# A smaller edge matrix and one-hots for four groups at once, in a four-layer graph network on one core

## The chip, the cores and the metric

The kernel runs on one core of a Trainium2 chip. Its time is the device time of one execution in microseconds (us); three executions of the kernel before took 3287.37, 3274.63 and 3283.2 us, a median of 3283.2 us. All rows of the profile come from one further execution that the hardware profiler recorded.

## What is computed

The reference runs four graph layers over 6250 nodes of 128 features and 106250 edges, which are sorted by their destination. Each layer is followed by a residual addition and a layer norm:

```python
x = _layernorm(x + _L0_gnn_ref(x, edge_attr_128, src, dst, ...))   # sums of edge features per destination, two dense layers
x = _layernorm(x + _L1_gnn_ref(x, edge_index, ...))                # sums of neighbours' rows, two dense layers with batch norms
x = _layernorm(x + _L2_gnn_ref(x, edge_index, ...))                # means of neighbours' rows, twice
x = _layernorm(x + _L3_gnn_ref(x, edge_index, edge_attr_16, ...))  # attention over the edges, three heads
```

What matters here is one expression. It is needed three times (once in the second layer and twice in the third):

```python
agg = jax.ops.segment_sum(x[src], dst, num_segments=n)
```

For each destination the rows of all its sources are added up, 17 on average. The edges are the same each time; only x differs.

## The kernel before

**Two ways to the sums.** The destinations are divided at ND = 5000 (line 45). For the first 5000 the kernel multiplies by a matrix: entry (s, d) is the number of edges from node s to destination d. It is built once, in bf16, kept in DRAM in ND/500 = 10 parts of 500 destinations ("edges", the list `matrix`), and read back by each of the three neighbour sums. For the other 1250 destinations the sources' rows are fetched from a table in DRAM, one indirect DMA of GpSimd (POOL) for 128 edges, and multiplied by one-hots of the destinations. The edges of these are in window groups of three such tiles; four groups make a quad, and the fetched quads are those from Q0 = 54 on: 183 tiles.

**Stage 0, the keys (to 101 us).** For each edge slot `key` gets a number that tells the block of the source and its destination within a group of GD = 5, and `low` the place of the source within its block. A group of five destinations fills one column of both tiles.

**Stage 1, layer 0's edge sums and the build (101 to 517 us).** The loop over `batches` (70) loads four window groups of edge features, makes their one-hots on VectorE (`one_hots`, line 352), multiplies them on TensorE (`by_group`, line 341), moves the result by ScalarE (line 343), and adds it to the layer's sums on VectorE (line 348). From the seventh batch on each turn advances `making` (from line 610) by some steps. One step of it is four groups: for each group VectorE compares a row of numbers with one column of `low` (`olow`, 128 wide, line 632) and another with one column of `key` (`okey`, 250 wide, line 634), TensorE multiplies the two one-hots (`made`, line 635), which counts the edges of 128 sources-in-block by 250 (block, destination) pairs, and ScalarE casts the four results from PSUM into the stage in the arena (line 637). 50 groups make a slice of SC = 250 destinations, that is 13 steps, the last with two groups; two slices make a part. A finished slice goes to DRAM in five DMAs on ScalarE's queue (line 618), 625 KB each. The pool `mk`, from which `olow` and `okey` come, has 8 buffers of each.

**Stages 2 to 4, `neighbours` (from line 770), called once for each sum.** Its outer loop runs over the matrix's parts, its inner one over ten pieces of each part. A piece is a DMA of 625 KB on SyncE's queue (five buffers) and 15 matmuls (line 837: five blocks by three, since the bf16 rows are split into three terms). After a piece, the generator `gathered` is advanced where the list `due` names that piece, so that the quads of the fetched destinations are spread over the pieces. One quad issues the fetches of the next quad (12, line 792; the `rows` pool holds two quads), makes one-hots, multiplies 24 times (`both`), and adds the result to `accg`. The spreading is in two lines:

```python
last = n_pieces * after // dense - 6
due = [(i + 2) * last // (2 * len(quads) + 2) for i in range(2 * len(quads))]
```

`after` is the number of parts after which the quads' destinations are finished (`others`): all of them in the first two calls, all but two in the third. `before`, `take`, `then` and `late` are the layer's own work on a part of 500 destinations, and `each` is work that is done once for a piece. In the first call `each` advances generators that load the 16-wide edge features on POOL's queue (lines 683 and 685, `eat`) and count edges (`counting`, lines 522 to 545, with an iota on POOL at line 540); in the second call it issues 50 indirect DMAs on POOL's queue (`last_sums`, line 657, `st`). In the third call `then` scatters each part's `edst` by four indirect DMAs on POOL's queue (line 1063).

**Stage 5, the attention (2300 to 3562 us),** gathers from x and uses neither the matrix nor the one-hots of the build.

What sets the order: each engine runs its instructions in the order in which the program issues them. POOL issues all indirect DMAs and works through them one by one; a fetch for quad q+1 can start when TensorE has used the rows of quad q-1.

Of the kernel before, what the change touches and what calls it, by code (L numbers as in the profile page):

```python
# [8 lines left out]
F32 = mybir.dt.float32  # L9
I32 = mybir.dt.int32  # L10
AF = mybir.ActivationFunctionType
OP = mybir.AluOpType
# [7 lines left out]
F = 128  # L20
# [18 lines left out]
RT, RB = 7, 119  # L39
GT, NG, GW = 3, 277, 32  # L40
BT, NBT, BW = 4, 208, 40
PB, NB5 = 125, 50
GD = 5
SC = 250
ND, Q0 = 5000, 54
AN = N - ND + SC + GW
BF16 = mybir.dt.bfloat16
ROUND = 12582912.0
# [7 lines left out]
def gnn_kernel(ctx: ExitStack, tc: tile.TileContext, a: dict, out: bass.AP):  # L56
# [142 lines left out]
    with tc.If(ordered) as cond:  # L199
        by_windows(tc, a, out, consts, ix)  # L200
# [9 lines left out]
def by_windows(ctx: ExitStack, tc: tile.TileContext, a: dict, out: bass.AP, consts, ix):  # L210


    nc = tc.nc
    iota, part, ident, ones, epst = consts
# [103 lines left out]
    def bases(at, n, engine, last=N - 1):  # L318

        got = {}  # L320

        def of(g):
            if g % 4 == 0:
                m = min(4, n - g)
                _, v = nc.values_load_multi_w_load_instructions(
                    ix["base"][0:1, at + g:at + g + m], engines=[engine], min_val=0, max_val=last,
                    skip_runtime_bounds_check_because=WITHIN)
                got.update({g + i: y for i, y in enumerate(v)})
            return got[g]
        return of  # L330
# [29 lines left out]
    arena = wide.tile([128, 2 * NB5 * SC], BF16, name="arena")  # L360
# [10 lines left out]
    def split(x, blocks, pool):  # L371
# [13 lines left out]
    keep = ExitStack()  # L385
    keyp = keep.enter_context(tc.tile_pool(name="keys", bufs=1))
    GP = 1024
    key = keyp.tile([128, GP], F32, name="key")
    low = keyp.tile([128, GP], F32, name="low")
    iob = keyp.tile([128, 128], BF16, name="iob")  # L390
    nc.vector.tensor_copy(iob, iota)
    iok = keyp.tile([128, NB5 * GD], BF16, name="iok")
    nc.gpsimd.iota(iok, pattern=[[1, NB5 * GD]], base=1, channel_multiplier=0,
                   allow_small_or_imprecise_dtypes=True)
    GC = GP // 128

    eap = keep.enter_context(tc.tile_pool(name="ea", bufs=4))
    ohp = keep.enter_context(tc.tile_pool(name="oh", bufs=3))
    mkp = keep.enter_context(tc.tile_pool(name="mk", bufs=8))
    evp = keep.enter_context(tc.tile_pool(name="ev", bufs=2))  # L400
    gw = keep.enter_context(tc.tile_pool(name="gw", bufs=1))
    pp = keep.enter_context(tc.tile_pool(name="sps", bufs=2, space=bass.MemoryType.PSUM))
# [24 lines left out]
    def start_row(r0, tg):  # L427
        nc.vector.tensor_scalar(r0, tg, 128.0, -128.0, op0=OP.mult, op1=OP.add)
        nc.vector.tensor_scalar(r0, r0, 0.0, float(E - 128), op0=OP.max, op1=OP.min)
# [9 lines left out]
    def by_c(x):  # L439
# [9 lines left out]
                   allow_small_or_imprecise_dtypes=True)  # L449
# [4 lines left out]
    for c in range(GC):  # L454
        for k in range(RT):
            nc.tensor.matmul(counts[:, c:c + 1], lhsT=below[:, k, c * 128:(c + 1) * 128], rhs=oneb,
                             start=(k == 0), stop=(k == RT - 1))
# [6 lines left out]
    s = gw.tile([128, GC], F32, name="s")  # L464
# [19 lines left out]
    s = a["L3_gnn_att_edge"]  # L484
# [12 lines left out]
    for cs in HALVES:  # L497
# [14 lines left out]
        for x, to in ((hi, key), (sf, low)):  # L512
            for c0 in range(cs.start, cs.stop, 4):
                n = min(4, cs.stop - c0)
                p = mps.tile([128, 4, 256], F32, name="made")
# [4 lines left out]
    M = 5  # L520

    def counting(pool, psum):


        row = tail[:RB, AN:AN + M * PB]
        view = arena[:RB, NB5 * 3 * F + 2 * (AN + M * PB):]
        steps = NB5 // M
        for c in range(steps + 1):
            if c:
                cs = slice((c - 1) * M, c * M)  # L530
                below = view[:, (c - 1) % 2 * M * PB:((c - 1) % 2 + 1) * M * PB]
                p = psum.tile([128, 2 * SC], F32, name="hp1")
                for i in range(M):
                    nc.tensor.matmul(p[:PB, i:i + 1], lhsT=below[:, i * PB:(i + 1) * PB], rhs=oneb,
                                     start=True, stop=True)
                start_row(n0[:PB, cs], p[:PB, 0:M])
                nc.vector.tensor_copy(n0i[:PB, cs], n0[:PB, cs])
            if c < steps:
                below = view[:, c % 2 * M * PB:(c % 2 + 1) * M * PB]
                nc.gpsimd.iota(row, pattern=[[1, M * PB]], base=c * M * PB + 1, channel_multiplier=0,  # L540
                               allow_small_or_imprecise_dtypes=True)
                nc.vector.tensor_scalar(below, row, ix["df"][:, 0:1], None, op0=OP.is_gt)
                for k in range(1, RT):
                    nc.vector.scalar_tensor_tensor(below, row, ix["df"][:, k:k + 1], below, op0=OP.is_gt, op1=OP.add)
            yield
# [34 lines left out]
    def products():  # L580
# [26 lines left out]
        nc.vector.tensor_add(cb, p, linb)  # L607
        yield

    def making(pool, psum):  # L610


        per = SC // GD
        full_of = []

        def store(i):
            s, w = full_of[0], NB5 * SC // 5
            nc.scalar.dma_start(matrix[s // 2][s % 2, :, i * w:(i + 1) * w],
                                stage[:, s % 2, :, :].rearrange("p h c -> p (h c)")[:, i * w:(i + 1) * w])
            if i == 4:  # L620
                full_of.pop()

        for s in range(ND // SC):
            for q in range(0, per, 4):
                if full_of and q // 4 in (1, 3, 5, 7, 9):
                    store(q // 8)
                n = min(4, per - q)
                p = psum.tile([128, 4, 256], F32, name="made")
                for i in range(n):
                    g = s * per + q + i  # L630
                    o = pool.tile([128, 128], BF16, name="olow")
                    nc.vector.tensor_scalar(o, iob, low[:, g:g + 1], None, op0=OP.is_equal)  # L632
                    w = pool.tile([128, NB5 * GD], BF16, name="okey")
                    nc.vector.tensor_scalar(w, iok, key[:, g:g + 1], None, op0=OP.is_equal)  # L634
                    nc.tensor.matmul(p[:, i, 0:NB5 * GD], lhsT=o, rhs=w, start=True, stop=True)  # L635
                to = stage[:, s % 2, :, q * GD:(q + n) * GD].rearrange("p h (i d) -> p i h d", d=GD)
                nc.scalar.copy(to, p[:, 0:n, 0:NB5 * GD].rearrange("p i (h d) -> p i h d", d=GD))  # L637
                yield
            full_of.append(s)
        for i in range(5):  # L640
            store(i)
# [53 lines left out]
    ea = a["edge_attr_128"]  # L695
    of = bases(0, NG, DVE)
    make = making(mkp, mps)
    product = products()
    quads, batches, LATE = ND // SC * 13, (NG + 3) // 4, 6
    for q in range(batches):  # L700
# [4 lines left out]
        n = min(4 * GT * 128, E - e0)  # L705
# [7 lines left out]
        p = pp.tile([128, F], F32, name="sums")  # L713
# [14 lines left out]
    with tc.tile_pool(name="l0w", bufs=2) as work, \  # L728
# [5 lines left out]
        for blocks in CHUNKS:  # L734
            b0, nb = blocks[0], len(blocks)
            w = nb * PB
# [16 lines left out]
            for j in range(nb):  # L753
                for m in range(4):
                    nc.tensor.matmul(yp[:PB, j, :], lhsT=ht[:, m, j * PB:(j + 1) * PB], rhs=w2[:, m, :],
                                     start=(m == 0), stop=(m == 3))
# [103 lines left out]
    with tc.tile_pool(name="l1", bufs=1) as wp:  # L860
# [5 lines left out]
        s = a["L1_gnn_eps"]  # L866
# [31 lines left out]
        with tc.tile_pool(name="l1d", bufs=1) as dp, tc.tile_pool(name="l1e", bufs=4) as two, \  # L898
                tc.tile_pool(name="hps", bufs=4, space=bass.MemoryType.PSUM) as hps:
            def take(k, p):  # L900
                nc.vector.scalar_tensor_tensor(h0[:, cols(k)], xt[:, cols(k)], eps1, p, op0=OP.mult, op1=OP.add)

            def then(k):
                for m in range(2):
                    stats(s1[:, m], k, hidden(k, m, hps))

            logit, indices = logits(dp, two), counting(dp, hps)

            def each(i):
                if i % 7 == 1:  # L910
                    next(indices, None)
                if i % 3 == 2:
                    next(logit, None)

            neighbours(None, take, then, tables[0], len(matrix), each)
            for x in (logit, indices):
                for _ in x:
                    pass
# [3 lines left out]
        with tc.tile_pool(name="l1p", bufs=1) as lp, tc.tile_pool(name="l1w", bufs=2) as work, \  # L922
# [4 lines left out]
            for k in range(len(PARTS)):  # L927
                h = work.tile([128, 2, 2 * SC], F32, name="h1")
                x = h0[:, cols(k)]
                w = x.shape[1]  # L930
# [11 lines left out]
        with tc.tile_pool(name="l1x", bufs=2) as work, tc.tile_pool(name="zps", bufs=3, space=bass.MemoryType.PSUM) as zps, \  # L942
                tc.tile_pool(name="tps", bufs=2, space=bass.MemoryType.PSUM) as tp:
            last = None
            for blocks in CHUNKS:
# [3 lines left out]
                                               op0=OP.mult, op1=OP.add)  # L949
# [961 lines left out]
```

## Time and profile before

| what | value |
|---|---|
| median of three timed executions | 3283.2 us |
| the profiled execution, and its span | 3564.17 us, 3562.0 us |
| granted TensorE clock over the span | 0.83 |
| stage 1 (keys ready to the last part written) | 101 to 517 us |
| first, second and third neighbour sum, with what is computed on them | 680 to 1062, 1204 to 1713, 1717 to 2184 us |
| attention | 2300 to 3562 us |

The profiled execution took 281 us longer than the median, so its rows are read for their proportions as well as for their durations. The costliest groups of instructions that the change touches:

```profile
L837 PE MATMUL sums<-piece,arena 125*128 125x500 bf16 x4500 | 1033.2, 384 | 66.3 <-issue 55.4
...
L792 POOL DMA_INDIRECT row<-table,srca x549 | 542.2, 988 | 317.8 <-issue 140.2
...
L637 ACT CAST arena<-made 128x1000 bf16<-128x1000 f32 (+1 forms) x260 | 313.5, 1261 | 61.3 <-PE made L635 52.7
...
L635 PE MATMUL made<-okey,olow 128*128 128x250 bf16 x1000 | 250.4, 329 | 59.5 <-ACT arena L637 26.2
L634 DVE TENSOR_SCALAR okey<-iok,key 128x250 bf16<-128x250 bf16 x1000 | 287.7, 288 | 0.0
...
L632 DVE TENSOR_SCALAR olow<-iob,low 128x128 bf16<-128x128 bf16 x1000 | 252.8, 253 | 0.0
```

A row names the line, the engine, the operation, the tiles written and read, the size and the number of instructions; then the busy time of all (us) and the mean of one (ns); then the engine's idle time before them, with what ended most of it. PE is TensorE, DVE VectorE, ACT ScalarE, POOL GpSimd and SP SyncE. The DMA issues of the edge matrix are these:

```profile
piece<-edges SPq DMA_DIRECT2D x300, 625.0 KB
edges<-arena ACTq DMA_DIRECT2D x100, 625.0 KB
```

### The profile page before, as it was taken

Reading aid. Unit: us, or ns where it says so; the run is one execution under the profiler, and the core shown is the slowest. Engines: PE = TensorE matmul, PEld = TensorE weight load, DVE = VectorE, ACT = ScalarE, POOL = GpSimd, SP = SyncE. Lnnn points to the kernel's source line nnn. Section 1 sums busy time; section 2 is a strip of 40 time slices with the busy share of each in tenths; the row PEclk is TensorE's granted clock in tenths of the full one; section 3 lists DMA queues with packets and bytes.
Section 4 is the critical chain, followed back from the end, with each engine's and each line's share of the span. In section 5 each row is a group of like instructions: output and inputs, shape, how many; then the busy total and the mean of one; then the engine's idle time right before and its main releaser. Section 6 shows DMA issues by size and latency. Waiting matters only on the chain.

```text
span 3562.0 us, 44386 instructions
## 1 busy us (share of the span) xinstructions
PE 2686.3 (75%) x14960; PEld 1638.6 (46%) x14960; DVE 1840.3 (52%) x6114; ACT 912.8 (26%) x1661; POOL 1693.8 (48%) x1689
## 2 busy tenths in 40 slices
PE   2788879799996479999787895566666666766665
PEld 1343436444443234445343342455555555655555
DVE  4999985387217400000211122666666666666666
ACT  0678864200005100001100010122222222222222
POOL 4000001277606475440466524666666666666663
PEclk8677789999997579999898997777777777777778
DMA  5588861387642346654454554122222222222221
GB/s 166 194 277 277 276 225 42 108 259 230 214 153 66 94 109 213 186 185 122 151 177 152 173 174 118 50 60 56 60 59 58 57 57 57 59 60 56 58 59 38
DMA packets 334840, 461.91 MB, mean 130 GB/s; under 512 B 45310, under 2 KB 219166, under 8 KB 334245
## 3 DMA queue, kind: packets, MB, share of 16 engines
q1 hardware_dynamic: 251420, 278.88, 26.0%
q0 software_dynamic: 54912, 105.86, 11.2%
q10 hardware_dynamic: 28270, 74.24, 5.7%
q8 instruction: 120, 1.97, 0.2%
q14 instruction: 118, 0.97, 0.1%
HBM read 375.30 MB, written 83.36 MB: 129 GB/s over the span
## 4 chain that ended last, share of the span: by engine, by line
PE 38%; DVE 10%; issue 10%; POOL 4%; another core or an unknown queue 3%; DMA 2%; ACT 1%; DVEq 0%; ACTq 0%; SPq 0%; POOLq 0%
PE sums L837 16%; PE o L1190 9%; PE w_p L1168 4%; PE o L1140 2%; POOL row L792 2%; DVE mx L1171 1%; PE yp L1012 1%; DVE w L1178 1%; POOL st L657 1%; PE both L1175 1%; DVE w L1163 1%; PE fp L1124 1%; PE both L341 1%; ACT w L1180 1%
## 5 line engine op out<-in xcount | busy, mean ns | idle before, releaser
L837 PE MATMUL sums<-piece,arena 125*128 125x500 bf16 x4500 | 1033.2, 384 | 66.3 <-issue 55.4
L1082 POOL DMA_INDIRECT rows<-x,srca x831 | 863.2, 1039 | 452.5 <-issue 215.1
L837 PEld LDWEIGHTS <-arena 125*128 125x128 bf16 x4500 | 436.6, 98 | 617.5 <-issue 153.9
L792 POOL DMA_INDIRECT row<-table,srca x549 | 542.2, 988 | 317.8 <-issue 140.2
L1190 PE MATMUL o<-rows,w 128*120 128x132 f32 x2078 | 406.5, 340 | 153.9 <-issue 78.6
L1190 PEld LDWEIGHTS o<-rows,w 128*120 128x120 f32 x2078 | 355.9, 239 | 192.6 <-issue 97.2
L637 ACT CAST arena<-made 128x1000 bf16<-128x1000 f32 (+1 forms) x260 | 313.5, 1261 | 61.3 <-PE made L635 52.7
L1180 ACT ACTIVATE w<-w 128x720 f32<-128x720 f32 x208 | 167.0, 803 | 610.0 <-DVE w L1178 464.8
L635 PE MATMUL made<-okey,olow 128*128 128x250 bf16 x1000 | 250.4, 329 | 59.5 <-ACT arena L637 26.2
L634 DVE TENSOR_SCALAR okey<-iok,key 128x250 bf16<-128x250 bf16 x1000 | 287.7, 288 | 0.0
L1171 DVE TENSOR_REDUCE mx<-w_p 120x1 f32<-120x768 f32 x208 | 198.0, 952 | 172.9 <-PE o L1190 76.0
L632 DVE TENSOR_SCALAR olow<-iob,low 128x128 bf16<-128x128 bf16 x1000 | 252.8, 253 | 0.0
L1168 PE MATMUL w_p<-ident,w 128*120 128x128 f32 x1248 | 231.0, 328 | 13.1 <-issue 6.3
L1178 DVE TENSOR_TENSOR w<-w,both 128x720 f32<-128x720 f32 x208 | 187.0, 899 | 81.5 <-PE w_p L1168 46.9
L352 DVE TENSOR_TENSOR onehot<-iota,relg 128x384 f32<-128x384 f32 x118 | 64.2, 546 | 309.2 <-PE both L341 183.3
L1175 PE MATMUL both<-ident,mx 120*128 120x120 f32 x208 | 74.5, 358 | 194.5 <-DVE acc L1198 121.8
L343 ACT COPY by_node<-both 128x128 f32<-128x128 f32 (+1 forms) x48 | 12.7, 266 | 810.5 <-PE both L341 531.3
L1168 PEld LDWEIGHTS w_p<-ident,w 128*120 128x120 f32 x1248 | 187.4, 169 | 56.8 <-issue 22.1
L635 PEld LDWEIGHTS <-olow 128*128 128x128 bf16 x1000 | 107.5, 113 | 184.7 <-DVE okey L634 91.2
L1163 DVE TENSOR_TENSOR w<-oh,z 128x720 f32<-128x720 f32 x208 | 187.3, 901 | 9.6 <-PE o L1190 8.3
L708 POOL MEMSET ea<- 128x128 f32 x1 | 0.5, 533 | 397.8 <-PE sums L341 397.8
L1140 PE MATMUL o<-zeros 128*120 128x380 bf16 x416 | 143.0, 396 | 23.9 <-issue 9.7
(286 smaller groups left out, 3308.6 us busy)
## 6 DMA issues: line engine op xcount, KB each, us to landing
piece<-edges SPq DMA_DIRECT2D x300, 625.0 KB
edges<-arena ACTq DMA_DIRECT2D x100, 625.0 KB
ea<-in_edge_attr_dram SPq DMA_DIRECT2D x69, 768.0 KB
loop<-x SPq DMA_DIRECT2D x208, 68.0 KB
rows<-x,srca POOLq DMA_INDIRECT x831
row<-table,srca POOLq DMA_INDIRECT x549
eat<-in_edge_attr_dram POOLq DMA_DIRECT2D x28, 236.0 KB
table<-xn SPq DMA_DIRECT2D x24, 224.0 KB
```

The source lines that it names most:

```text
L632: nc.vector.tensor_scalar(o, iob, low[:, g:g + 1], None, op0=OP.is_equal)
L634: nc.vector.tensor_scalar(w, iok, key[:, g:g + 1], None, op0=OP.is_equal)
L635: nc.tensor.matmul(p[:, i, 0:NB5 * GD], lhsT=o, rhs=w, start=True, stop=True)
L637: nc.scalar.copy(to, p[:, 0:n, 0:NB5 * GD].rearrange("p i (h d) -> p i h d", d=GD))
L792: nc.gpsimd.indirect_dma_start(out=r[:, j, :], out_offset=None, in_=table, in_offset=bass.IndirectOffsetOnAxis(ap=ix["src"][:, t:t + 1], a ...
L837: nc.tensor.matmul(p, lhsT=xp[:PB, h, i, :], rhs=t[:PB, :, (h - h0) * SC:(h - h0 + 1) * SC], start=(h == 0 and i == 0), stop=(h == NB5 - 1 ...
L1082: nc.gpsimd.indirect_dma_start(out=r[:, j, :], out_offset=None, in_=x3, in_offset=bass.IndirectOffsetOnAxis(ap=ix["src"][:, BT * b + j:BT ...
L1163: nc.vector.tensor_tensor(w, oh.to_broadcast([128, S, H, BW]), z.rearrange("p j (h w) -> p j h w", w=1).to_broadcast([128, S, H, BW]), op= ...
L1168: nc.tensor.transpose(tp[:, j // 3, j % 3 * 128:(j % 3 + 1) * 128], w[:, j, :, :].rearrange("p h w -> p (h w)"), ident)
L1171: nc.vector.tensor_reduce(mx, tp[:, :, 0:384], AX.XY, OP.max)
L1178: nc.vector.tensor_tensor(wf, wf, mb.rearrange("p (j h) w -> p j (h w)", j=1) .to_broadcast([128, S, H * BW]), op=OP.subtract)
L1190: nc.tensor.matmul(o[:, 0:F + H + 1], lhsT=wf[:, j, :], rhs=rr, start=(j == 0), stop=(j == S - 1))
```

## The change

The matrix covers 4500 destinations in nine parts, and the rows of 1750 are fetched: from quad 49 on, 243 tiles for each sum instead of 183. The fetched destinations' sums `accg` are 500 columns wider. In the build, the one-hots of four groups are made by one comparison of two bf16 operands (tensor_tensor) in place of four comparisons of a bf16 row with one fp32 number in each partition (tensor_scalar). Element (m, i) of the new tile is for number m and group i, so that the four groups' values lie side by side; a matmul then reads every fourth element of a row. The row of numbers is laid out to match, and `key` and `low` become bf16, which holds their whole numbers exactly. The pool `mk` has three buffers instead of eight, each for four groups. `counting` gets buffers of its own in place of a stretch of the arena.

```diff
-ND, Q0 = 5000, 54
+ND, Q0 = 4500, 49
...
-    key = keyp.tile([128, GP], F32, name="key")
-    low = keyp.tile([128, GP], F32, name="low")
-    iob = keyp.tile([128, 128], BF16, name="iob")
-    nc.vector.tensor_copy(iob, iota)
-    iok = keyp.tile([128, NB5 * GD], BF16, name="iok")
-    nc.gpsimd.iota(iok, pattern=[[1, NB5 * GD]], base=1, channel_multiplier=0,
+    key = keyp.tile([128, GP], BF16, name="key")
+    low = keyp.tile([128, GP], BF16, name="low")
+
+    iob = keyp.tile([128, 128, 4], BF16, name="iob")
+    nc.gpsimd.iota(iob, pattern=[[1, 128], [0, 4]], base=0, channel_multiplier=0,
+                   allow_small_or_imprecise_dtypes=True)
+    iok = keyp.tile([128, NB5 * GD, 4], BF16, name="iok")
+    nc.gpsimd.iota(iok, pattern=[[1, NB5 * GD], [0, 4]], base=1, channel_multiplier=0,
                    allow_small_or_imprecise_dtypes=True)
...
-    mkp = keep.enter_context(tc.tile_pool(name="mk", bufs=8))
+    mkp = keep.enter_context(tc.tile_pool(name="mk", bufs=3))
...
-        view = arena[:RB, NB5 * 3 * F + 2 * (AN + M * PB):]
+        view = pool.tile([RB, 2 * M * PB], BF16, name="below2")
...
+    def hots(pool, name, numbers, of):
+
+        m, n = numbers.shape[1], of.shape[1]
+        o = pool.tile([128, m, 4], BF16, name=name)
+        nc.vector.tensor_tensor(o[:, :, 0:n], numbers[:, :, 0:n],
+                                of.rearrange("p (o g) -> p o g", o=1).to_broadcast([128, m, n]), op=OP.is_equal)
+        return o
+
...
+                g = s * per + q
+                o = hots(pool, "olow", iob, low[:, g:g + n])
+                w = hots(pool, "okey", iok, key[:, g:g + n])
                 for i in range(n):
-                    g = s * per + q + i
-                    o = pool.tile([128, 128], BF16, name="olow")
-                    nc.vector.tensor_scalar(o, iob, low[:, g:g + 1], None, op0=OP.is_equal)
-                    w = pool.tile([128, NB5 * GD], BF16, name="okey")
-                    nc.vector.tensor_scalar(w, iok, key[:, g:g + 1], None, op0=OP.is_equal)
-                    nc.tensor.matmul(p[:, i, 0:NB5 * GD], lhsT=o, rhs=w, start=True, stop=True)
+                    nc.tensor.matmul(p[:, i, 0:NB5 * GD], lhsT=o[:, :, i], rhs=w[:, :, i], start=True, stop=True)
```

## The prediction

> **What bounds the kernel now.** I read the 40 slices first (89 us each), since the shares over the whole span mix stages.
>
> ```profile
> PE   2788879799996479999787895566666666766665
> ...
> DVE  4999985387217400000211122666666666666666
> ACT  0678864200005100001100010122222222222222
> POOL 4000001277606475440466524666666666666663
> PEclk8677789999997579999898997777777777777778
> DMA  5588861387642346654454554122222222222221
> ```
>
> See three kinds of stage: one where DVE shows 9 (slices 2 to 5), a middle with PE at 7 to 9 and POOL at 4 to 7, and a long end in which nothing is full. The timeline puts them at 101 to 517 us (layer 0's edge sums, with the matrix built beside them), 680 to 1062, 1204 to 1713 and 1717 to 2184 (layers 1 to 3), and 2300 to 3562 (attention, which the change does not touch). The table by windows (PE, DVE, ACT, POOL busy, clock, DMA share, GB/s) gives the limits:
>
> ```profile
> 200.00:300.00 100.00, 80.28 (x637) 39.93 (x627) 99.79 (x562) 78.74 (x80) 0.00 (x0) 0.78 0.85 278
> 300.00:400.00 100.00, 80.97 (x624) 40.41 (x627) 99.94 (x563) 79.69 (x79) 0.00 (x0) 0.73 0.83 273
> ...
> 682.00:1062.00 380.00, 362.53 (x1963) 166.38 (x1963) 178.04 (x313) 4.25 (x16) 221.04 (x244) 0.97 0.69 217
> ...
> 1310.00:1510.00 200.00, 197.37 (x1033) 97.81 (x1033) 17.95 (x55) 14.52 (x32) 104.13 (x107) 0.98 0.59 188
> ...
> 1717.00:2069.00 352.00, 288.76 (x1523) 130.35 (x1524) 59.94 (x222) 22.62 (x51) 207.07 (x218) 0.88 0.56 172
> ```
>
> In the build DVE is full, with PE, ACT and the DMA engines at four fifths: they stand close behind. Layer 2 is PE's. In layer 3 PE has 63 us idle, and the POOL rows below say why: an indirect fetch takes 0.95 us, and 0.30 us more pass before the next, so POOL's 207 busy us are nearly the whole stretch.
>
> ```profile
> 739.56 0.52 POOL L685 DMA_DIRECT2D eat<-in_edge_attr_dram  x1
> 740.38 1.15 POOL L792 DMA_INDIRECT row<-table,srca  x1 [0.30 <-PE sums L837]
> 741.84 0.97 POOL L792 DMA_INDIRECT row<-table,srca  x1 [0.30 <-issue]
> ```
>
> The releaser changes from row to row while the 0.30 stays, so it is a cost of each fetch, not a wait. Layer 1 is balanced: its quads' products start every 20.3 us on PE (a quad: the products L341 of four window groups), and twice PE already waits for rows:
>
> ```profile
> 837.19 0.86 PE L341 MATMUL both<-row,onehot 128*32 128x128 f32 x24 [1.40 <-issue]
> ...
> 863.67 1.08 PE L341 MATMUL both<-row,onehot 128*32 128x128 f32 x16 [4.37 <-issue]
> ```
>
> **Part 1, the one-hots (gain of the build).** Today each group of five destinations costs DVE an olow and an okey:
>
> ```profile
> 299.85 0.24 DVE L632 TENSOR_SCALAR olow<-iob,low 128x128 bf16<-128x128 bf16 x1
> 300.01 0.28 DVE L634 TENSOR_SCALAR okey<-iok,key 128x250 bf16<-128x250 bf16 x1
> 300.21 0.24 DVE L632 TENSOR_SCALAR olow<-iob,low 128x128 bf16<-128x128 bf16 x1
> ```
>
> Start to start that is 0.36 us, so 1.44 us for four groups and 360 us for 1000; the other 55 us of DVE's 416 are the edge sums' own. Afterwards two tensor_tensor make four groups, of 512 and 1000 elements. No bf16 tensor_tensor is in the trace. The nearest rows are fp32 ones:
>
> ```profile
> L352 DVE TENSOR_TENSOR onehot<-iota,relg 128x384 f32<-128x384 f32 x118 | 64.2, 546 | 309.2 <-PE both L341 183.3
> ```
>
> With 240 elements at 398 ns and 720 at 901 that is 1.05 ns an element, and the next starts some 75 ns before the recorded end. At that rate (one bound) the pair takes 0.60 + 1.11 = 1.71 us, more than the 1.44 it replaces. The rule that speaks against the change is in the Trainium skill, "VectorE: DVE Perf Modes", The perf-mode tier table: bf16 tensor_scalar has a four-element mode, tensor_tensor stops at two. The trace fits the first half: olow and okey differ by 122 elements and 35 ns, 0.29 ns each. Read alone it says that elements get dearer, 378 x 4 at 0.29 (0.44 us) becoming 1512 at 0.52 (0.79). But eight fixed costs become two: today's 1.44 less 0.44 is 1.0 us of fixed cost, afterwards it is two of about 0.07 (the fp32 rows' intercept less the overlap). That gives 0.93 us. I take 0.93, because the operands have what the two-element mode asks (all two bytes, last step one), and keep 1.71 as the other end. 234 sets of four or fewer groups (nine parts instead of ten) then cost DVE 218 us, with its other 55: 273.
>
> What is late next? **ACT's cast**, back to back:
>
> ```profile
> 402.26 1.30 ACT L637 CAST arena<-made 128x1000 bf16<-128x1000 f32 x1 [0.57 <-PE made L635]
> ...
> 403.42 1.30 ACT L637 CAST arena<-made 128x1000 bf16<-128x1000 f32 x1
> ```
>
> Every 1.16 us: 234 of them 271, and 61 by_node copies of 0.27 bring 287. PE is busy 80.5% of 416, 335 us, less 100 made matmuls at 329 ns: 302. DMA: the windows' rates from 101 to 517 make 106 MB; less 6.25 for the tenth part 99.5 MB, at 278 GB/s over 0.85 (327 with all engines busy) 304 us, at 278 itself 358. Three resources at 287 to 304 that pass work to each other through two PSUM buffers and three one-hot buffers (three hold three sets; eight held two) don't all reach full: I take 302/0.87 = **350 us, 66 less**, bounds 325 and 400.
>
> PE now reads its weights and columns at steps of 8 bytes, which no row of the trace shows. Bounds: nothing, or half rate: a made matmul back to back takes 107 ns, so +107 x 900 at a clock of 0.75, 128 us of PE, and the stage about 430. By the Trainium skill, "SBUF — State Buffer", Door 1 (its note on cachelines), a line has 16 bytes and two reads of a line suffice for full rate; 8 bytes give two. I take nothing, keeping part of the other in the range.
>
> Head: POOL makes iob (512) and a wider iok on the chain there, about 1.2 us by iok's 0.35 for 250 elements; DVE loses the copy. The ACT queue issues 90 stores instead of 100, counted in the DMA sum. The own buffer for `below` adds no instruction.
>
> **Part 2, 4500 instead of 5000.** Each layer does 1350 matrix matmuls, not 1500, and reads 56.25 MB, not 62.5 (90 SP issues). A piece of 15 matmuls takes 3.17 us (start to start 0.211). It fetches 243 tiles, not 183, and has five quads more of 24 products (0.86 us, about 1.0 with the transposes). One-hots for five more quads (5 x 0.55 us of DVE) and a memset longer by 0.45 us lie beside PE.
>
> Layer 2: PE-bound from 1310. Ten pieces less is -31.7, five quads +5, one late part moved into the block after the last quad (about 7.5 us, part of it there before) +3.6: **-23**. POOL's 12 fetches of 1.25 us per quad (15.2) stay under PE's new 16.5 us.
>
> Layer 1: PE's period falls from 20.3 to 13.9 us (3.8 pieces and products per quad). POOL's is 12 x 1.33 = 16.0 (the rows longer than 0.95 included), and before its last fetches it issues 45 eat loads and 11 memsets at 0.55 and ten iotas at 0.68, about 40 us. So PE waits for rows from now on: from 680, 240 x 1.30 + 40 = 352, the last full quad at about 1036; then 14 pieces (44) and the last quads' remains (6): 1086 against 1062, **+24** (15 to 30). If POOL were no limit: -32 + 5 + 4, -23.
>
> Layer 3: POOL-bound already. 60 fetches more at 1.25 are +75; about four scatters (1.2 us, 0.3 and 2 of waiting for the one before) fall behind the gather, -13; the 8.2 us for which POOL here waits for L341 go, -8; then 32 pieces instead of 35, -9.5, and one part more in the block after the gather, +3: **+48** (20 to 60). SP's piece loads have five buffers and run ahead; they don't bind in either.
>
> Sum against the profiled 3564.2: -66 + 24 - 23 + 48 + 2 = **-15**. The timed median, 3283.2, is 0.92 of that execution; I can't see where the 281 us lie, so I scale: -14, **3269 us**.
>
> **Rivals.** (A) is this sum: what DVE gives up, POOL takes back.
> (B) Fetches are cheaper in timed runs: if the 0.30 us is mostly the recording's, layer 1 is PE's (-23) and layer 3 gains less time than feared (60 x 0.95 less 22: +35): -66 - 23 - 23 + 35 + 2 = -75, scaled 3214. For it: 8% between profile and median. Against: nothing shows that they lie here.
> (C) On the other side: the new comparison runs one element a cycle. Place: the build; price: (234 x 1.71 + 55) - 416 = +39; with the rest +90, 3366. For it: the only rows; against: the mode's conditions hold. It decides from 1.33 us a pair on: there the stage takes 365 us, and its 51 us equal what layers 1 to 3 lose.
> (D) What stands behind DVE binds at once (strided reads on PE, DMA share 0.85): only 25 us: +26, 3307. For it: three neighbours at 80%; against: none is above 304 us.
>
> **How the numbers follow.** A 0.40, B 0.18, C 0.18, D 0.24. A's own range is 3235 to 3300. A measurement of this kernel can tell 0.5%, 16 us, from no change. A's centre lies just inside: half of A is faster, 0.14 the same, 0.06 slower; B is faster but 0.01; C slower; D 0.03 the same. Faster 0.38, same 0.19, slower 0.43. The range takes half of B and the nearer half of C: 3195 to 3345.
>
> **What would show it.** Right: DVE below 85% in the build and its end near 450; ACT L637 near 1.2 us apart; PE in layer 1 idle before L341 with POOL's fetches without a gap but 0.30; the last L341 of layer 3 some 55 us later against the layer's start. Wrong: a DVE row of 1000 elements near 1.18 us (C); made matmuls longer than 329 ns on average (D); L341 in layer 1 every 14 us (B).

## The result, and the profile after

The changed kernel takes 3278.26 us, the kernel before 3278.53 us (medians of 12 executions each): a ratio of 1.0007, 95% interval 0.9992 to 1.0023. There is no difference that can be measured. On one of the chips used here the kernels take about 10% longer (3594.84 us for the kernel before), and the execution that the prediction was worked from, of 3564 us, is like those, so a second profile of the kernel before (span 3268.4 us) is used from here on, and the ratio of an experiment is to the kernel before on the same chip.

The slices of the changed kernel's profile are 82 us each:

```profile
PE   3899999686998385999877668556666766666665
...
DVE  4888744586315800111211113176777787777776
ACT  0788854000004300001300001023323233333333
POOL 5000020677746277773177762467777777777773
PEclk5798889798999587999988789878888898888888
DMA  6699931676661353776355455422323332323331
```

In the build (slices 2 to 5) DVE has gone from 9 to 8 and 7, PE stands at 8 and 9, and DMA reaches 9. In the three sums (slices 8 to 26) POOL stands at 7 in ten slices, where it did in three in the prediction's profile. The table by windows shows the same stages of both kernels. The columns are the stretch, its length, busy us of PE, its weight loads, DVE, ACT and POOL (each with its count), the granted clock, DMA share and GB/s. The kernel before, second profile: build, first, second and third sum with what is computed on each, attention:

```profile
96.00:514.00 418.00, 340.12 (x2527) 167.05 (x2525) 414.14 (x2320) 328.63 (x323) 0.35 (x1) 0.74 0.76 252
678.00:1191.00 513.00, 442.32 (x2201) 211.17 (x2201) 283.94 (x646) 65.79 (x125) 289.57 (x302) 0.90 0.59 178
1191.00:1673.00 482.00, 439.36 (x2230) 217.35 (x2231) 52.95 (x140) 46.74 (x96) 230.94 (x233) 0.95 0.57 167
1673.00:2088.00 415.00, 372.81 (x2061) 178.96 (x2059) 83.09 (x338) 32.24 (x73) 232.10 (x251) 0.95 0.63 188
2088.00:3268.00 1180.00, 754.86 (x4917) 641.14 (x4915) 863.34 (x2305) 360.37 (x911) 850.53 (x836) 0.84 0.28 67
```

The changed kernel:

```profile
92.00:434.00 342.00, 310.67 (x2427) 158.50 (x2425) 278.24 (x793) 289.44 (x297) 0.20 (x1) 0.86 0.88 290
598.00:1137.00 539.00, 424.76 (x2179) 203.04 (x2177) 302.12 (x692) 67.08 (x130) 349.79 (x361) 0.87 0.55 163
1137.00:1621.00 484.00, 420.71 (x2205) 207.83 (x2206) 59.00 (x165) 47.95 (x101) 286.86 (x293) 0.92 0.55 161
1621.00:2095.00 474.00, 363.00 (x2036) 172.15 (x2034) 89.06 (x366) 33.92 (x79) 288.02 (x311) 0.87 0.55 159
2095.00:3275.00 1180.00, 744.15 (x4915) 631.40 (x4915) 862.28 (x2303) 359.95 (x911) 852.61 (x836) 0.85 0.29 67
```

The lengths to a tenth, from the first and last starts of the tiles (the build: from its first made product to its last cast; the first sum: from its first product with the matrix to the first fetch of the second; the second: from there to the first fetch of the third; the third: from there to its last copy):

| stage | before | after | difference | predicted |
|---|---|---|---|---|
| build | 417.3 | 341.7 | -75.6 | -66 |
| first sum and what follows | 512.5 | 539.0 | +26.5 | +24 |
| second sum and what follows | 482.5 | 484.8 | +2.3 | -23 |
| third sum | 415.2 | 473.1 | +57.9 | +48 |
| all else (head, layer 0, attention) | 1440.9 | 1436.9 | -4.0 | +2 |
| span | 3268.4 | 3275.5 | +7.1 | -15 |

So large differences cancel: 76 us less in the build, 87 more in the sums. The two comparisons of the new build, from the timeline of VectorE (start, us):

```profile
250.61 0.42 DVE L616 TENSOR_TENSOR olow<-iob,low 128x512 bf16<-128x512 bf16 x1 [0.33 <-PE made L643]
250.95 0.67 DVE L616 TENSOR_TENSOR okey<-iok,key 128x1000 bf16<-128x1000 bf16 x1
251.54 0.55 DVE L352 TENSOR_TENSOR onehot<-iota,relg 128x384 f32<-128x384 f32 x1
```

Start to start they take 0.34 and 0.59, 0.93 us together; 488 elements more cost 0.25 us, 0.51 ns each. The bf16 comparison runs at twice the rate of the fp32 row. The first comparison had to wait 0.33 us for TensorE: VectorE no longer sets the pace.

### The profile page after: what moved, and what is told of

It is laid out like the page before. It is cut to its first block, busy times and chain, and to the rows that moved or that the text cites. A ratio compares the mean times of both kernels' runs of the same rounds, so it can differ in the third digit from the quotient of the medians.

```text
span 3275.5 us, 42858 instructions
## 1 busy us (share of the span) xinstructions
PE 2437.8 (74%) x14785; PEld 1487.7 (45%) x14785; DVE 1711.0 (52%) x4656; ACT 873.2 (27%) x1650; POOL 1848.3 (56%) x1870
## 4 chain that ended last, share of the span: by engine, by line
PE 26%; DVE 13%; issue 10%; POOL 9%; DMA 8%; ACT 2%; DVEq 1%; POOLq 0%; ACTq 0%; SPq 0%
PE sums L845 13%; PE o L1198 5%; DMA rows<-x,srca 4%; POOL rows L1090 4%; POOL row L800 3%; DVE w L1186 3%; DVE w L1171 3%; ACT w L1188 2%; DMA row<-table,srca 2%; POOL st L665 1%; PE yp L1020 1%; DVE mx L1179 1%; PE w_p L1176 1%; PE fp L1132 1%; PE both L341 1%
## 5 line engine op out<-in xcount | busy, mean ns | idle before, releaser
L845 PE MATMUL sums<-piece,arena 125*128 125x500 bf16 x4050 | 922.4, 384 | 4.3 <-DMA piece<-edges 4.3
L800 POOL DMA_INDIRECT row<-table,srca x729 | 708.6, 972 | 360.0 <-issue 171.4
L845 PEld LDWEIGHTS <-arena 125*128 125x128 bf16 x4050 | 393.5, 99 | 484.1 <-issue 69.1
L1198 PE MATMUL o<-rows,w 128*120 128x132 f32 x2078 | 357.1, 311 | 251.1 <-ACT w L1188 251.0
L1198 PEld LDWEIGHTS o<-rows,w 128*120 128x120 f32 x2078 | 306.0, 210 | 294.5 <-ACT w L1188 294.3
L341 PE MATMUL both<-row,onehot 128*32 128x128 f32 x1458 | 85.5, 315 | 226.8 <-DVE arena L348 125.5
L352 DVE TENSOR_TENSOR onehot<-iota,relg 128x384 f32<-128x384 f32 (+1 forms) x133 | 72.0, 544 | 297.4 <-PE both L341 288.8
L348 DVE TENSOR_TENSOR arena<-arena,both 128x32 f32 x243 | 45.2, 186 | 263.4 <-PE both L345 250.6
L341 PEld LDWEIGHTS both<-row,onehot 128*32 128x32 f32 x1458 | 45.7, 121 | 272.9 <-DVE arena L348 132.2
L616 DVE TENSOR_TENSOR okey<-iok,key 128x1000 bf16<-128x1000 bf16 (+1 forms) x234 | 152.4, 651 | 0.0
```

Of the source, the lines that this page charges most:

```text
L341: nc.tensor.matmul(p[i * GW:(i + 1) * GW, :], lhsT=oh[:, i * GT + j, :], rhs=rows[i][:, j, :], start=(j == 0), stop=(j == GT - 1))
L800: nc.gpsimd.indirect_dma_start(out=r[:, j, :], out_offset=None, in_=table, in_offset=bass.IndirectOffsetOnAxis(ap=ix["src"][:, t:t + 1], a ...
L845: nc.tensor.matmul(p, lhsT=xp[:PB, h, i, :], rhs=t[:PB, :, (h - h0) * SC:(h - h0 + 1) * SC], start=(h == 0 and i == 0), stop=(h == NB5 - 1 ...
L1198: nc.tensor.matmul(o[:, 0:F + H + 1], lhsT=wf[:, j, :], rhs=rr, start=(j == 0), stop=(j == S - 1))
```

## The experiments

**Each part alone.** The kernel before again, then the one-hots alone:

```diff
-ND, Q0 = 4500, 49
+ND, Q0 = 5000, 54
```

> The kernel before, unchanged, for a second profile. Theory: the first profile of it was of an execution in which the attention ran slower (1308 us from its first product against 1110 in the changed kernel, whose attention is the same code), so a new profile spans about 3280 us with an attention near 1110, and the stages ahead of it together are some 80 us shorter than in the first. If the build is then still about 410 us long, the change's gain there is real; rival: the build itself was disturbed and takes only 345 to 360 us, in which case the new one-hots gain next to nothing.

> The change's one-hots alone: the matrix stays at 5000 destinations and the fetched tiles at 183. Theory (two large parts that cancel): the build is shorter by about the 66 us of the prediction less one tenth of DMA work, so 3215 us (3200 to 3235), build 360 us. Rival (both parts are near nothing): 3265 to 3285 us.

The kernel before again: 0.9992 (0.9981 to 1.0003), with a build of 417.3 us; so the build was alike in the first profile (415.7), and it is later stages that were longer there, the attention most (1379 us after the third sum, 1180 here). The one-hots alone: 0.9874 (0.9857 to 0.989), 3232.19 us. The build takes 383.0 us, 34 less than before, the three sums 513.1, 484.2 and 416.9, as before within 2 us. The theory's 3200 to 3235 holds in the time, but the build came out 23 us longer than its 360. From there to the changed kernel the smaller matrix gives -41.3 in the build, +25.9, +0.6 and +56.2 in the sums: together +41. The two parts cancel almost exactly.

**The smaller matrix alone,** with the one-hots of before (`counting` gets its own buffer as in the change, since at 4500 the stretch of the arena that is left for it is too short):

```diff
-ND, Q0 = 5000, 54
+ND, Q0 = 4500, 49
...
-        view = arena[:RB, NB5 * 3 * F + 2 * (AN + M * PB):]
+        view = pool.tile([RB, 2 * M * PB], BF16, name="below2")
```

> 4500 destinations alone with the one-hots of before (and the buffers of counting of the change, which it needs for room). Theory (two large parts that cancel): the build, full on VectorE, loses a tenth of its comparisons, 417 to 380 us; the three neighbour sums gain the 84 us that they gained in the changed kernel: 3310 to 3325 us. Rival (the sums lengthen because of how the new build leaves the queues, not because of the fetches): 3240 to 3280 us.

1.0295 (1.0255 to 1.0334), on the slower chip. The build is 381.8 us, as expected. The ratio is worse than the 1.011 to 1.016 that the expected times are of 3273.55 us, since the sums lengthen more there: they take 573.2, 552.8 and 531.0 us, against 519.0, 519.0 and 462.9 in the first profile of the kernel before, which is of that chip's length. That is 156 us more, not 84. The rival, that they lengthen only with the new build, is out.

**What the new build waits for.** In the changed kernel the made products take longer than before, 400 ns in the mean instead of 332. The next kernel stores key and low twice, side by side, so that the comparison can write each group's one-hot packed and still has pairs of bf16 in its last step:

```diff
-    key = keyp.tile([128, GP], BF16, name="key")
+    key = keyp.tile([128, GP, 2], BF16, name="key")
...
-        o = pool.tile([128, m, 4], BF16, name=name)
-        nc.vector.tensor_tensor(o[:, :, 0:n], numbers[:, :, 0:n],
-                                of.rearrange("p (o g) -> p o g", o=1).to_broadcast([128, m, n]), op=OP.is_equal)
+        o = pool.tile([128, 4, m], BF16, name=name)
+        nc.vector.tensor_tensor(o[:, 0:n, :].rearrange("p g (m t) -> p g m t", t=2),
+                                numbers.rearrange("p (g m t) -> p g m t", g=1, t=2).to_broadcast([128, n, m // 2, 2]),
+                                of.rearrange("p g (m t) -> p g m t", m=1).to_broadcast([128, n, m // 2, 2]),
+                                op=OP.is_equal)
...
-                    nc.tensor.matmul(p[:, i, 0:NB5 * GD], lhsT=o[:, :, i], rhs=w[:, :, i], start=True, stop=True)
+                    nc.tensor.matmul(p[:, i, 0:NB5 * GD], lhsT=o[:, i, :], rhs=w[:, i, :], start=True, stop=True)
```

> One-hots for four groups by one comparison as in hots_5000, but written so that each group's one-hot is packed (key and low are stored twice, side by side, so that the comparison still has pairs of bf16 in its last step); TensorE then reads at steps of 2 bytes instead of 8. Theory (the 8-byte steps halve TensorE's rate in the made products, and TensorE at 90% busy is what bounds the new build): made products start 0.11 us apart instead of 0.22, their mean falls from 400 to about 290 ns, the build from 383 to 345-355 us, the whole from 3232 to about 3200. Rival (the casts with their two PSUM buffers, or the DMA engines at a share of 0.92, bound it): the build stays at 375-385 and the whole at 3225-3235.

> The changed kernel with packed one-hots (as packed_5000). Theory (TensorE's half-rate reading bounds the build): 342 us fall to 305-318, the 90 us that 900 products lose being only partly usable since the DMA engines are at a share of 0.98. Rival (at 4500 the DMA engines bound it already): 332-342 us.

> As packed_4500, but only okey (the moving operand of the made products) is packed; olow (the weights) keeps the change's steps of 8 bytes. Theory (the moving operand's reading halves the rate, the weights' doesn't matter): the made products have a mean near 290 ns and start 0.11 us apart, and the build takes 303-310 us as in packed_4500. Rival (both operands suffer, the weight load too): a mean of 320 or more, weight loads of 119 ns instead of 102, the build 315-342 us.

Packed at 5000: 0.9777 (0.9746 to 0.9808) on the slower chip, with a build of 338.4 us instead of the 383.0 of the one-hots alone (the build is alike on both chips: 341.7 us in the changed kernel, 340.8 in st_late_4500 below). Packed at 4500: 0.9903 (0.9876 to 0.9929), build 302.9 instead of 341.7. Both builds were below the theory's own figures. The third kernel packs okey, the moving operand, and leaves olow, the weights, as the change has it; it was timed once, at 3244.86 us, and its build takes 304.1. Groups of the made products in the changed kernel, in packed_4500 and in half_packed_4500:

```profile
L643 PE MATMUL made<-okey,olow 128*128 128x250 bf16 x900 | 232.6, 400 | 29.2 <-ACT arena L645 16.9 <-DVE olow L616 7.8 <-DVE okey L616 1.0
```

```profile
L647 PE MATMUL made<-okey,olow 128*128 128x250 bf16 x900 | 146.4, 287 | 76.0 <-ACT arena L649 57.7 <-DVE olow L618 6.1 <-DVE xt L348 3.7
```

```profile
L655 PE MATMUL made<-okey,olow 128*128 128x250 bf16 x900 | 145.8, 287 | 77.7 <-ACT arena L657 61.8 <-DVE okey L618 4.2 <-DVE olow L628 4.0
```

The mean falls by 113 ns, and four in a row take 0.59 us instead of 1.06; from TensorE's timeline, changed kernel and packed_4500:

```profile
251.98 1.06 PE L643 MATMUL made<-okey,olow 128*128 128x250 bf16 x4 [0.24 <-ACT arena L645]
```

```profile
302.45 0.59 PE L647 MATMUL made<-okey,olow 128*128 128x250 bf16 x4 [0.56 <-ACT arena L649]
```

With the last one's own length taken off, three starts take 0.66 us in the one and 0.32 in the other: 0.22 and 0.11 us apart. The 8-byte steps of the moving operand halve TensorE's rate. Those of the weights make a weight load longer (117 ns in the mean in half_packed_4500, 102 in packed_4500), but not the products (287 in both).

How much TensorE did in the build is told by the packed build's window, to be held against the 310.67 us of the changed kernel's, and by the made products of the old one-hots at 4500 (nd4500_old2):

```profile
99.00:402.00 303.00, 219.33 (x2424) 140.53 (x2423) 271.61 (x791) 277.92 (x298) 0.20 (x1) 0.93 0.98 327
```

```profile
L635 PE MATMUL made<-okey,olow 128*128 128x250 bf16 x900 | 227.1, 331 | 52.3 <-ACT arena L637 22.0 <-DVE okey L634 6.3 <-DVE olow L632 3.1
```

The same 900 products keep TensorE busy for 227 us when their one-hots come group by group, for 146 when four packed ones come at once, and for 233 when the four are strided. So four at once saved TensorE 81 us, and the strided reading took 86 of them back. The clock differs too (0.74, 0.93 and 0.86 in these builds), and no run parts its share in the 81.

What TensorE waits for in the packed build is ScalarE's cast (57.7 us), and the DMA share there is 0.98; which of the two bounds it was not tested. For the rival of the DMA engines this settles one thing: at the change's 290 GB/s they were not full, since the packed build moves 327 GB/s.

**Is POOL's queue the bound of the sums at 4500?** One third of the fetches are left out, the second tile of each group standing in for the third, so a third of the fetched edges' rows are missing from the result:

```diff
-                    for j in range(GT):
+                    for j in range(GT - 1):
...
-                nc.tensor.matmul(p[i * GW:(i + 1) * GW, :], lhsT=oh[:, i * GT + j, :], rhs=rows[i][:, j, :],
+                nc.tensor.matmul(p[i * GW:(i + 1) * GW, :], lhsT=oh[:, i * GT + j, :], rhs=rows[i][:, min(j, held - 1), :],
```

> The changed kernel with two of three tiles of each fetched group really fetched, the second one standing in for the third in the products: a third of the fetched edges' rows are left out of the result. TensorE, VectorE and the pieces do the same work; POOL issues 162 fetches for each sum instead of 243, fewer than the 183 of before. Theory (POOL's queue bounds the three sums at 4500): the first sum falls from 398 to 345-360 us, the second by 40-55, the third by 75-95, together 160-200 us. Rival (the additions at line 348 and the spacing of the quads over the pieces set the pace): together under 60 us.

> The changed kernel again, beside the others of this call. If the kernel before takes about 3275 us in this call, it is within 0.3% of it, as measured. If the kernel before takes about 3595, as in the call before this one, the sum of the stages seen there in the two kernels with 4500 destinations (first sum 443, second 655, third 569 us against 380, 621 and 501 of before; build 342 against 416) makes it about 1.5 to 2% slower.

The ratio is 0.9468 (0.9437 to 0.9499); the changed kernel, timed again beside it, has 1.0012 (1.0002 to 1.0022). Against that one (542.2, 485.0, 475.7 us) the sums take 481.8, 455.7 and 384.6: 60, 29 and 91 us less, 181 together of the expected 160 to 200. The first, measured to the end of its last product with the matrix, is 340.8 us long, just under the expected 345 to 360; the second gained less than its 40 to 55. TensorE's and VectorE's work is unchanged, so the fetches are what lengthens the first and third sum. The run leaves out their transfers together with their issues; the DMA share of 0.55 in these sums speaks for the issues.

Part of this reaches TensorE by a detour. Its waits for the additions at line 348 grew with the change, in the first sum from 15.0 to 52.1 us, and in the third as follows (the kernel before, second profile; the changed kernel; two_of_three):

```profile
PE both L341 <- DVE arena L348: 26.9, 4, 13.5
```

```profile
PE both L341 <- DVE arena L348: 73.4, 5, 21.7
```

```profile
PE both L341 <- DVE arena L348: 19.3, 3, 9.4
```

In the first sum these additions stand on VectorE's queue behind products of edge features, whose loads come over POOL's queue too. In the third they stand behind a step of the layer's own work on `xw`, which waits for a memset on POOL. From the changed kernel's timeline:

```profile
1729.69 1.20 POOL L1071 DMA_INDIRECT edst<-ad,start_of  x1 [0.30 <-issue]
1730.89 0.13 POOL L1048 MEMSET xw<- 128x20 f32 x1
1731.05 0.17 DVE L1066 TENSOR_TENSOR xw<-st,rcnt 125x12 f32<-125x12 f32 x1 [23.83 <-POOL xw L1048]
1731.21 0.19 DVE L348 TENSOR_TENSOR arena<-arena,both 128x32 f32 x1
1731.45 1.51 PE L341 MATMUL both<-row,onehot 128*32 128x128 f32 x24 [21.73 <-DVE arena L348]
```

A memset of 0.13 us had to wait for its turn behind fetches and scatters; VectorE waited 23.83 us for it, and TensorE 21.73. VectorE's waits of this kind did not grow with the change (136.7 us before, 130.6 after, 11 each); what grew is the part of them that TensorE feels. A memset on another engine was not tried, so what it alone would give is open.

A second try in the same direction moved the eat loads to SyncE's queue:

```diff
-            nc.gpsimd.dma_start(x[0:RB - 1], ea[0:full, :].rearrange("(p t) k -> p t k", t=L)[:, c:c + W, :])
+            nc.sync.dma_start(x[0:RB - 1], ea[0:full, :].rearrange("(p t) k -> p t k", t=L)[:, c:c + W, :])
...
```

> The changed kernel with the 56 loads of the 16-wide edge features (eat) issued on SyncE's queue instead of POOL's. Theory (POOL's queue bounds the first neighbour sum at 4500): about 45 of them leave that stage, 45 x 0.55 = 25 us less, the stage 375 instead of 399 us, the whole about 3253. Rival (TensorE's waits for VectorE's additions at line 348 are what lengthens it, and they come from VectorE's own work): within 5 us of the changed kernel.

1.026 (1.0221 to 1.0299), on the slower chip. The changed kernel itself was not timed there, but st_late_4500 below has the same first sum and was: 578.7 us there, 594.8 here. No gain, rather a loss. The table of waits for this sum says what took over:

```profile
POOL row L800 <- PE both L341: 51.1, 11, 10.7
```

```profile
PE sums L845 <- DMA piece<-edges: 28.2, 12, 4.2
```

POOL now waits for TensorE (51.1 us in 11 waits; 0.6 us in st_late_4500), and TensorE for the pieces (28.2 us), which share SyncE's queue with the moved loads. TensorE's waits for the additions at line 348 did fall, from 33.3 us in st_late_4500 to 10.7. So the loads had a part in those waits, but neither theory's number came: the jam only moved.

**Where the second sum's gain went.** The 50 st transfers are held behind the sum's last fetch. They are named from piece 76 on, and `issue_after` ties each to the last fetch:

```diff
+    fetched = [None]
...
-                        nc.gpsimd.indirect_dma_start(
+                        fetched[0] = nc.gpsimd.indirect_dma_start(
...
-        neighbours(before, take, None, tables[1], len(matrix), lambda i: next(ends, None))
+        def sums_of(i):
+            if i >= 76:
+                for _ in range(4):
+                    with tc.issue_after(fetched[0].ins):
+                        next(ends, None)
+
+        neighbours(before, take, None, tables[1], len(matrix), sums_of)
```

> The changed kernel with the 50 indirect DMAs of st in the second neighbour sum put behind the last fetch of that sum on POOL's queue. Theory (the predicted 23 us of that sum were lost because POOL bounds its first 150 us, where 50 x 1.5 us of st stand before the fetches): the 59 us for which TensorE waits for rows there nearly go, the whole 3225 to 3240. Rival (the spacing of the quads over the pieces sets the length, and st only fills POOL's spare time): within 8 us of the changed kernel.

1.0011 (0.9983 to 1.0039), on the slower chip, so the expected 3225 to 3240 us can't be held against it. Two other kernels timed there have the second sum of the changed kernel: 557.5 us (eat_sp_4500) and 552.8 (nd4500_old2). Here it is 494.2, some 60 us less. In the changed kernel POOL's timeline shows why:

```profile
1238.38 0.94 POOL L800 DMA_INDIRECT row<-table,srca  x1 [0.30 <-issue]
1239.63 0.94 POOL L800 DMA_INDIRECT row<-table,srca  x1 [0.30 <-issue]
1240.87 1.19 POOL L665 DMA_INDIRECT st<-esum,lasti  x1 [0.30 <-issue]
1242.37 1.21 POOL L665 DMA_INDIRECT st<-esum,lasti  x1 [0.30 <-issue]
```

A batch of 12 fetches is followed by a batch of st, 1.5 us each, while TensorE waits for rows. These waits over the second sum, in the kernel before (second profile) and in the changed one:

```profile
PE both L341 <- DMA row<-table,srca: 39.1, 13, 8.7
```

```profile
PE both L341 <- DMA row<-table,srca: 59.0, 22, 9.3
```

**A version that beats both, and the same at 4500.** 5000 destinations, packed one-hots, st late, and the edst scatters of the third sum collected and issued behind its last fetch in the same way (13 buffers for their source). The second kernel differs by ND and Q0 (and the piece from which st is issued).

```diff
-            ad = work.tile([128, 4, 4], F32, name="ad")
+            ad = adp.tile([128, 4, 4], F32, name="ad")
...
+            scatters.append((ad, b0, nb))
...
+        neighbours(None, take, then, tables[2], len(matrix) - 2)
+        for ad, b0, nb in scatters:
             for j in range(nb):
...
+                with tc.issue_after(fetched[0].ins):
+                    nc.gpsimd.indirect_dma_start(
```

> What the runs so far point to: 5000 destinations, packed one-hots, st behind the last fetch of the second sum, and the edst scatters of the third sum behind its last fetch (their source tiles get 13 buffers). Theory: against the kernel before, build -77 us, second sum -30 to -40 (TensorE waits 38 us for rows there), third -25 to -45 (POOL spends about 35 scatters of 1.5 us and their waits inside the gather, TensorE waits 37 us): 0.95 to 0.96 of its time. Rival for the scatters: pushed to the end they hold up the attention's first fetches on the same queue, and the third sum's gain is given back there.

> best_5000 with 4500 destinations. Theory (POOL bounds the three sums at 4500 even when st and edst are out of its way: 243 fetches of 1.25 us are 304 us for each sum, against 229): the build is 34 us shorter than best_5000's, the first sum 27 longer, the second 0-15, the third 30-45, so 25-50 us slower than best_5000: 0.967 to 0.974 of the kernel before. Rival (once st and edst are late, the fetches fit beside TensorE's work and the smaller matrix pays): 0.945 to 0.957.

0.9592 (0.9566 to 0.9619), 3140.07 us, and 0.966 (0.9643 to 0.9676), 3160.86 us. At 5000, against the second profile of before: build -80.8, first sum -4.4, second -36.0, third -10.4. The scatters gave less than the expected 25 to 45: the third sum's last fetch comes 48 us sooner in the stage, but 167 us are left after it, not 130, with TensorE 140 of them busy. The attention is not held up (1176 us after the third sum, 1180 before). The windows of the second sum, at 5000 and at 4500:

```profile
1104.00:1551.00 447.00, 432.34 (x2236) 216.35 (x2236) 52.80 (x140) 47.16 (x97) 239.36 (x250) 0.98 0.62 183
```

```profile
1102.00:1523.00 421.00, 405.11 (x2209) 204.77 (x2209) 59.26 (x165) 48.45 (x101) 293.30 (x309) 0.98 0.62 188
```

TensorE is 97% and 96% busy: with st out of the way the second sum is TensorE's, and the smaller matrix makes it 25.4 us shorter. At 4500 it takes 421.1 us, where the changed kernel's takes 484.8. The expectation of 0 to 15 longer was wrong there. The first sum is 27.8 us longer at 4500 and the third 54.6, the build 34.3 shorter. The time lay just under the theory's band and well above the rival's.

## Why the prediction was right

The forecast of 3269 us held (3278.26 measured), and by its own mechanism: rival A, a build that gains what POOL takes back. It had given a time that can't be told from the old one the least chance of the three outcomes (0.19; the parts that it lists add up to 0.18, with 0.37 for faster and 0.45 for slower). Step by step:

- **The comparison** was forecast at 0.93 us for four groups and took 0.93, by the terms forecast: 0.51 ns an element for 0.52, and two fixed costs in place of eight. The four-element mode of tensor_scalar was no argument against the change, as weighed: VectorE's busy time in the build fell from 414 to 278 us, for 273 forecast. Rival C is out.
- **TensorE's reading** was taken at nothing, on the word of the Trainium skill ("SBUF — State Buffer", Door 1), and the other bound, half rate, is what was measured: 0.22 us apart, and a mean of 400 ns, which the prediction had named as a sign of rival D. For the moving operand the measurement contradicts that note; strided weights took 15 ns more to load and did not slow the products. This term was wrong; it costs 39 us of the build at 4500 (341.7 to 302.9).
- **The build** still gained 75.6 us, more than the 66 forecast, and here luck had a part. TensorE's 302 us kept the old 329 ns for every made product. Four at once saved 81 us of TensorE's time (the clock's share in it included), which the prediction did not see, and half rate cost 86, which it took at nothing: 311 us were measured. That is also why its 430 us for half rate did not come: it set 128 us on top of 302. The other miss is 0.87, the share that the busiest engine was expected to reach; TensorE reached 0.91. TensorE's busy share doesn't order the granted clocks (0.81 at a clock of 0.74 before, 0.91 at 0.86 after, 0.72 at 0.93 packed), and what raised the clock was not tested.
- **The first sum**, +24 forecast, +26.5 measured; two_of_three shows that the fetches make it. The last fetch was forecast 352 us after the sum's start and came after 353.
- **The second sum** was forecast at -23 and came out at +2.3. The step that failed is "POOL's 12 fetches of 1.25 us per quad (15.2) stay under PE's new 16.5 us": it counted from 1310 us on and left the first 110 us of that sum, in which 50 st of 1.5 us stand between the fetches (1194 to 1315 us in the prediction's profile). With st late, the pair best_5000 and best_4500 shows -25.4: the sum for TensorE was right, and what was missing was the queue.
- **The third sum**, +48 forecast, +57.9 measured, inside its bounds of 20 to 60. The sign and the cause held; the size was off by 10 us, and the traces place it. From the first fetch to the last the sum is 58 us longer (285.7 to 343.8), for 54 forecast: the 8.2 us of waits for L341 that were to go are 1.5 in the second profile. Behind the last fetch 6.5 us were to go, and the stretch stayed at 129. The reading that POOL's 207 us are "nearly the whole stretch" was too strong: with 218 pauses of 0.30 they make 272 of 352, and in the rest POOL waits, for TensorE and for a scatter before the next one.
- **The scaling by 0.92** rested on the assumption that the 281 us were spread over all stages. They were not: the build was alike in both profiles, and 199 us lay behind the third sum, in which the change has no part. It moved the centre by 1 us only.

The terms missed by -10 us (build), +3, +25 and +10 (the sums) and -6 (all else), 22 together, well within the range of 150. Rival B is out: its ground was that the recorded execution was 8% longer than the timed ones, and the second profile (3268.4 us) is as long as they are (3269.89 in the median); in two_of_three the timed median falls by 180 us, as the profiled sums do. Of D, the strided reading was real, and its price was hidden behind what TensorE saved.

## What to carry to other kernels

When work moves from one resource to another, count the receiving queue in each stage, over the whole stage and with everything else that is issued on it; a queue that is free in the second half of a stage is not free in the first, and a memset of 0.13 us on it can hold up two other engines. An operand layout that suits the engine that writes it must also be priced at the engine that reads it: here a comparison that writes packed rows costs VectorE the same, and the products that read them start at half the distance. And take a second profile before explaining where a recorded execution is longer than the timed ones.

## What the runs showed of the hardware

- A bf16 comparison of two operands, one of them a row of four repeated over 250 numbers, took 0.67 us for 1000 elements and 0.42 for 512; with pairs repeated in place of fours (packed_4500) the same 0.67 and 0.41 to 0.42.
- 250 columns of a moving bf16 operand at steps of 8 bytes start 0.22 us apart, packed ones 0.11. Weights at 8-byte steps: 117 ns for a load instead of 102, and no difference in the made products (287 ns in the mean either way).
- In every profile an indirect fetch of 128 rows holds POOL for 0.95 us in the median, and 0.30 us pass before the next, an indirect st for 1.2 us with the same 0.30. An edst scatter takes 1.2 us too, and in the median 1.6 us or more before it, in which it waits for the one ahead.
